# Two routing groups for three, a reordered start and end, and the first layernorm split between ScalarE and VectorE, in a fused attention and mixture-of-experts layer

## The chip, the cores and the metric

The kernel runs on one core of a Trainium2 chip. The metric is the device time of one execution in microseconds (us), the median of several runs. All data is float32.

A core has five engines that work side by side and wait for each other by semaphores: TensorE (PE, matmuls; PEld is its weight load), VectorE (DVE), ScalarE (ACT), GpSimd (POOL) and SyncE (SP, which here only issues transfers). Each works through its own queue in order, so an instruction that waits holds up all that stand behind it. Matmuls write PSUM; everything else lives in SBUF.

## The reference

x has 16 sequences of 512 tokens of 128 numbers (8192 tokens, 64 tiles of 128). Two layers follow each other, with a layernorm around each:

```python
q = silu(x @ Wq); k = silu(x @ Wk); v = x @ Wv        # 16 heads of 8
q, k = lrpe(q, theta), lrpe(k, theta)                 # [t*cos(theta*n), t*sin(theta*n)]
energy = einsum('bhnd,bhmd->bhnm', q, k) * tril       # causal, without a softmax
out = (energy @ v).reshape(b, n, d) @ Wo * sigmoid(x @ G1 @ G2)
out = (out - mean) / sqrt(var + 1e-5) * gamma + beta  # the first layernorm
x = layernorm(x + out)                                # the second
# mixture of experts: 8 experts, 2 for each token, 1280 places for each expert
shared = silu(x @ sg) * (x @ su) @ sd                 # 128 -> 1024 -> 128, all tokens
routed = the same form with 512 hidden, for the tokens of each expert, weighted, added back
x = layernorm(x + shared + routed)
```

## The kernel before

**First part: the loop over tiles.** Lines 788 to 832 go over t = -2 to 64, one tile of 128 tokens at a time. An iteration projects tile t+2 (`project`, L414: two matmuls L418 and L421 into one PSUM tile; SiLU, tanh and spreading copies on ScalarE, L425 to L441; the multiplication with cosines and sines on VectorE, L445), transposes tile t+1 (`turn_over`, L458, with four copies on ScalarE), computes the products of queries and keys of tile t (`energies`, L505, masked on VectorE, L513), the outputs of tile t-1 (`values`, L530 and L538, copied at L544), and adds tile t+1 to a running state (`remember`, L479; VectorE masks it at L488, POOL adds it at L490). Linear attention lets it carry a state instead of all earlier keys.

When the four tiles of a sequence are through, a generator `after(b)` (L547) is started. It projects with Wo (L553), gates (L557), takes the statistics of the first layernorm (L105, L107, L111; POOL raises to the power -1/2, L113), applies it with two groups of four VectorE instructions (L565, L570), and does the second layernorm (statistics, L580, and ScalarE's L584). Then it transposes the result into x1T (L600, L601) and computes the router's logits. Each `yield` in it ends one slot; `advance` runs one slot at two places of each iteration.

The shared expert is a list of 384 small steps (`feed`), 24 for each sequence: eight of `gate_half` (L137, L139) and eight of `up_half` (L150, L151), a 512-wide matmul each, and eight of `down_half` (L160, and L165 for every second one). `shared(t)` takes the next step if its sequence is released (`ready[b]`), twice an iteration. They fill TensorE's queue.

Routing (`route`, L618) runs once for each group of sequences. It is a chain of some 40 VectorE instructions over all tiles of the group, with one Exp on ScalarE (L644, which loads another activation table) and two matmuls (L690, L691). `sprinkle` deals its slots out. At its end every tile of the group owes two scatters: each an indirect transfer that POOL issues (L723), writing 128 token rows to the places of their experts in DRAM. Before a scatter, `beat` (L740), a tiny POOL instruction that reads a recent result, holds POOL back. The loop issues two scatters a tile.

After tile 64 a second loop (L838 to L856) goes on with shared steps alone, one an iteration, until the last sequences are finished, routed and scattered, with one scatter every second iteration, and 12 steps more.

**Second part.** The eight experts (L1021 to L1026, L928 to L942) load their rows (`load_expert`), blank rows that nobody filled (`clear_rows`, L893), transpose them (L904, L905) and scatter results back. What is left of `feed` then fills TensorE while, for each sequence, the two results of its tokens are loaded (`load_pair`) and added (`add_up`, L953), and the last layernorm is taken over lots of tiles (`finish_lot`, L969: L105, L107, a root, L985, ScalarE's L988, and the store). The lots are the four tiles of a sequence, single tiles for the last one.

The order of instructions on TensorE, ScalarE, VectorE and POOL is the order in which the code issues them (`manual_schedule`).

Of the kernel before, what the change touches and what calls it, by code (L numbers as in the profile page):

```python
# [13 lines left out]
ALU = mybir.AluOpType  # L14
# [33 lines left out]
def tile_kernel(  # L48
# [145 lines left out]
    groups = [(0, 6), (6, 12), (12, 16)]  # L194
    with ExitStack() as ph:
# [21 lines left out]
        with tc.manual_schedule(engines=ORDERED):  # L217
            th_row = cst.tile([1, D + HALF], F32, name="th_row")
            nc.sync.dma_start(th_row, theta.unsqueeze(0))
# [15 lines left out]
            nc.vector.memset(half_pi, math.pi / 2)  # L235
            warm = cst.tile([P, 1], F32, name="warm")
# [25 lines left out]
            nc.vector.tensor_scalar(rowi, rowi, 16, None, ALU.bitwise_and)  # L262
            bitf = cst.tile([P, 1], F32, name="bitf")
            nc.vector.tensor_copy(bitf, rowi)
            par = cst.tile([P, 2], F32, name="par")
            nc.vector.tensor_scalar(par[:, 0:1], bitf, -1.0 / 16, 1.0, ALU.mult, ALU.add)
            nc.vector.tensor_scalar(par[:, 1:2], bitf, 1.0 / 16, None, ALU.mult)
# [11 lines left out]
            pth = ps_w.tile([P, D + HALF], F32, tag="w", name="pth")  # L279
            nc.tensor.matmul(pth, ones[0:1, :], th_row, start=True, stop=True)  # L280
            th_sb = wk1.tile([P, D + HALF], F32, tag="w", name="th_sb")
            nc.scalar.copy(th_sb, pth)
# [3 lines left out]
            for vp in vpads[2:]:  # L286
                nought(vp.rearrange("p a b d -> p (a b d)"), 640)
# [3 lines left out]

            cst_tok = cst.tile([P, NC, 2, 16, 2, 8], F32, name="cst_tok")
            scratch = hp.tile([P, 10, D + HALF], F32, tag="h", name="scratch")
            turns_of = wk1.tile([P, D + HALF], F32, tag="o", name="turns_of")
            nc.vector.tensor_scalar(turns_of, pth, 1.0 / (2.0 * math.pi), None, ALU.mult)

        def angles(c, th):

            a, size, k, whole = scratch[:, c], scratch[:, NC + c], scratch[:, 8], scratch[:, 9]
            both = ((slice(0, D), pos[:, 0, c : c + 1]), (slice(D, D + HALF), pos[:, 1, c : c + 1]))
            for m, at in both:
                nc.vector.tensor_scalar(k[:, m], turns_of[:, m], at, MAGIC, ALU.mult, ALU.add)
            nc.vector.tensor_scalar(whole, k, MAGIC, -C1, ALU.subtract, ALU.mult)
            for m, at in both:
                nc.vector.scalar_tensor_tensor(a[:, m], th[:, m], at, whole[:, m], ALU.mult, ALU.add)
            nc.vector.tensor_scalar(k, k, MAGIC, -C2, ALU.subtract, ALU.mult)
            nc.vector.tensor_tensor(a, a, k, ALU.add)
            nc.vector.scalar_tensor_tensor(size, a, -1.0, a, ALU.mult, ALU.max)  # L310
            nc.vector.tensor_scalar(a, a, -PI_BELOW, PI_BELOW, ALU.max, ALU.min)
# [4 lines left out]
        def sines(c):  # L316

            for s, (from_, scale, bias) in enumerate([(scratch[:, NC + c], -1.0, half_pi), (scratch[:, c], 1.0, 0.0)]):
# [14 lines left out]
        with tc.manual_schedule(engines=ORDERED):  # L333
            angles(0, pth)
            sines(0)
            angles(1, th_sb)
            same(0)

# [3 lines left out]
            nc.gpsimd.tensor_tensor(causal[:, 0:1], scratch[:, 0, 0:1], zcol, ALU.mult)  # L342
# [13 lines left out]
            for at in (0, HALF):  # L356
                rows = causal[at : at + HALF, :]
                nc.gpsimd.affine_select(
                    rows, rows, pattern=[[1, HALF]], compare_op=ALU.is_ge, fill=0.0, base=0, channel_multiplier=-1
                )  # L360
# [53 lines left out]
        def project(t):  # L414
# [27 lines left out]
            if 0 < t < NC:  # L442
                same(t)
# [669 lines left out]
```

## Time and profile before

| what | value |
|---|---|
| median of 3 runs | 866.24 us (865.83 to 866.31) |
| the profiled execution | 866.67 us, of which its span 864.9 us |
| TensorE busy | 821.7 us (95%) |
| VectorE, ScalarE, POOL busy | 538.2 (62%), 414.5 (48%), 361.6 us (42%) |
| granted TensorE clock, mean | 0.988 |
| tiles: first projection to last (L418) | 5.0 to 358.1 us |
| last scatter issued (L723) | 521.6 us |
| experts (L1021, L1023) | 536.5 to 750.6 us |
| last matmul (L160) ends | 856.4 us |

A row of the profile by groups reads: line, engine and operation, the names out<-in with shapes, how often; busy time in us and mean duration in ns; idle time of the engine just before, and what ended it. A row of a timeline begins with start and duration in us; a wait stands in brackets at its end. A row of waits reads: who waited for whom, total us, how often, longest. Busy time by stage has the stretch, its length, then busy time and instructions of each engine, and the granted clock (PEclk, 1.00 is full speed).

### The profile page before, as it was taken

The page shows a single profiled execution, that of the slowest core. Times are in us where ns is not written, and L with a number is a line of the kernel's source. Part 1 is how long each engine was busy: PE and PEld are TensorE (multiplying, and loading weights), DVE is VectorE, ACT ScalarE, POOL GpSimd, SP SyncE. Part 2 cuts the span into 40 slices and gives each one's busy share as a digit, 9 for nine tenths or more (in the row PEclk, how much of TensorE's full clock was granted, in tenths as well). Part 3 has the DMA queues.
Part 4 walks back from the last instruction along what each step waited for, and adds up shares of the span by engine and source line. Part 5 has one row for each costly group of instructions (what it writes and reads, how often), then busy time and mean ns, then how long its engine had stood idle before and what let it go on. Part 6 is the DMA issues. An engine that isn't in the chain of part 4 may idle for free. (4 is left out here: it accounts for less than half of the span.)

```text
span 864.9 us, 25793 instructions
## 1 busy us (share of the span) xinstructions
PE 821.7 (95%) x10288; PEld 559.5 (65%) x10288; DVE 538.2 (62%) x1695; ACT 414.5 (48%) x1342; POOL 361.6 (42%) x512
## 2 busy tenths in 40 slices
PE   6899999989999999999999999999999999999996
PEld 4666667657766765756666656766777667765564
DVE  7688887789877778865533324434344444268864
ACT  5676776676566567534222221333333333324445
POOL 2233333332366676677666671333343333412110
PEclk9899999999999999999999999999999999999998
DMA  6011111111111110039000005122321210046512
GB/s 199 22 35 33 33 33 34 33 34 33 38 43 55 55 47 22 22 130 326 28 14 8 1 1 152 37 90 91 95 84 35 90 61 28 27 143 182 155 49 62
DMA packets 66395, 57.55 MB, mean 67 GB/s; under 512 B 6180, under 2 KB 55132, under 8 KB 66274
## 3 DMA queue, kind: packets, MB, share of 16 engines
q1 hardware_dynamic: 59474, 44.95, 17.0%
q0 software_dynamic: 6656, 10.69, 3.8%
q8 instruction: 81, 1.33, 0.7%
q10 hardware_dynamic: 144, 0.26, 0.1%
q14 instruction: 40, 0.33, 0.1%
HBM read 32.62 MB, written 26.48 MB: 68 GB/s over the span
## 5 line engine op out<-in xcount | busy, mean ns | idle before, releaser
L723 POOL DMA_INDIRECT xg_dram<-x,idx x128 | 128.9, 1007 | 38.7 <-issue 34.1
L934 POOL DMA_INDIRECT y_dram<-y,to x80 | 77.5, 969 | 158.4 <-ACT y L932 158.4
L151 DVE TENSOR_TENSOR h<-sl,pu 128x512 f32<-128x512 f32 x128 | 87.8, 686 | 80.9 <-PE pu L150 45.5
L137 PE MATMUL pg<-x1T,sg_sb 128*128 128x512 f32 x256 | 131.5, 595 | 1.7 <-DVE x1T L165 1.7
L139 ACT ACTIVATE sl<-pg 128x512 f32<-128x512 f32 x128 | 75.5, 594 | 119.6 <-PE pg L137 73.4
L150 PE MATMUL pu<-x1T,su_sb 128*128 128x512 f32 x256 | 130.8, 593 | 0.0
L160 PE MATMUL pd<-sd_sb,h 128*128 128x128 f32 x1024 | 122.8, 276 | 4.7 <-DVE x1T L165 4.7
L160 PEld LDWEIGHTS pd<-sd_sb,h 128*128 128x128 f32 x1024 | 119.1, 192 | 11.5 <-issue 5.7
L1026 DVE TENSOR_TENSOR eh<-esl,peu 128x512 f32<-128x512 f32 (+1 forms) x96 | 57.5, 599 | 109.7 <-PE peu L1023 96.5
L113 POOL TENSOR_TENSOR rstd<-ve,neghalf 128x4 f32<-128x4 f32 x45 | 49.3, 1095 | 125.4 <-DVE ve L111 121.0
L490 POOL TENSOR_TENSOR state<-state,add 128x128 f32<-128x128 f32 x96 | 44.1, 459 | 137.4 <-DVE add L488 131.0
L928 PEld LDWEIGHTS ped<-rd,eh 128*128 128x128 f32 x640 | 84.0, 192 | 24.6 <-issue 22.5
L513 DVE TENSOR_TENSOR et<-pe,causal 128x256 f32<-128x256 f32 x256 | 90.5, 416 | 14.5 <-PE pe L505 13.0
L1021 PE MATMUL peg<-xgT,rg 128*128 128x512 f32 (+1 forms) x192 | 84.6, 522 | 0.0
L1023 PE MATMUL peu<-xgT,ru 128*128 128x512 f32 (+1 forms) x192 | 84.4, 521 | 0.0
L928 PE MATMUL ped<-rd,eh 128*128 128x128 f32 x640 | 84.3, 275 | 0.0
L1025 ACT ACTIVATE esl<-peg 128x512 f32<-128x512 f32 (+1 forms) x96 | 50.5, 526 | 55.0 <-PE peg L1021 52.3
L150 PEld LDWEIGHTS pu<-x1T,su_sb 128*128 128x128 f32 x256 | 45.7, 190 | 44.1 <-issue 38.7
L932 ACT ACTIVATE y<-ped,wt 128x128 f32<-128x128 f32 x80 | 29.4, 368 | 84.6 <-PE ped L928 84.6
L137 PEld LDWEIGHTS pg<-x1T,sg_sb 128*128 128x128 f32 x256 | 44.3, 191 | 38.9 <-issue 33.7
L418 PE MATMUL pq<-W,xT 128*128 128x384 f32 x128 | 61.0, 560 | 4.7 <-ACT qT L467 2.5
L445 DVE TENSOR_TENSOR hat<-qk,cst_tok 128x512 f32<-128x512 f32 x64 | 44.9, 702 | 26.2 <-ACT qk L427 26.1
(176 smaller groups left out, 1272.0 us busy)
## 6 DMA issues: line engine op xcount, KB each, us to landing
y_dram<-vpad SPq DMA_DIRECT2D x16, 512.0 KB
y<-y_dram SPq DMA_DIRECT2D x32, 256.0 KB
xT<-xt SPq DMA_DIRECT2D x15, 384.0 KB
xg<-xg_dram SPq DMA_DIRECT2D x8, 660.0 KB
x<-x SPq DMA_DIRECT2D x16, 256.0 KB
o<-res SPq DMA_DIRECT2D x15, 256.0 KB
xg_dram<-x,idx POOLq DMA_INDIRECT x128
rg<-rg SPq DMA_DIRECT2D x8, 256.0 KB
```

The costliest lines, as they stand in the source:

```text
L137: nc.tensor.matmul(pg, sg_sb[:, ts(i, P)], seq, start=True, stop=True)
L139: nc.scalar.activation(sl, pg, AF.Silu)
L150: nc.tensor.matmul(pu, su_sb[:, ts(i, P)], seq, start=True, stop=True)
L151: nc.vector.tensor_tensor(h[i // half][:, i % half, :], h.pop(("s", i)), pu, ALU.mult)
L160: nc.tensor.matmul(pd, h[k][:, i - k * half, ts(c, P)], sd_sb[:, i, :], start=(i == 0), stop=(i == IS // P - 1))
L418: nc.tensor.matmul(pq[:, :, 0:24], xts[b][:, c, 0:P], W[:, 0:384].rearrange("p (h n) -> p h n", n=24), start=True, stop=True)
L513: nc.vector.tensor_tensor(et.rearrange("p s i n -> p (s i) n"), pes[a, half].rearrange("p s i n -> p (s i) n"), causal.unsqueeze(1).to_bro ...
L723: i = nc.gpsimd.indirect_dma_start(out=xg_dram[:, :], out_offset=bass.IndirectOffsetOnAxis(ap=idx[:, k, t : t + 1], axis=0), in_=x1[:, t, ...
L928: nc.tensor.matmul(pd, h[:, i, ts(c, P)], got[e][2][:, i, :], start=(i == 0), stop=(i == IR // P - 1))
L934: i = nc.gpsimd.indirect_dma_start(out=y_dram[:, :], out_offset=bass.IndirectOffsetOnAxis(ap=to[:, at : at + 1], axis=0), in_=y, in_offset ...
L1021: nc.tensor.matmul(pg[:, :n], rg_sb[:, ts(i, P)], xgTs[e][:, ds(o0, n)], start=True, stop=True)
L1023: nc.tensor.matmul(pu[:, :n], ru_sb[:, ts(i, P)], xgTs[e][:, ds(o0, n)], start=True, stop=True)
```

## The change

Several parts at once. The groups become two of eight sequences. Constants for the start are computed by fewer VectorE instructions: ScalarE makes theta times position (`linear`) and the absolute value, and the first three tiles are laid out by hand in front of the loop, which now begins at t = 1. `project` is cut into pieces for that (`products`, `squash`, `gate`, `spread`, `turn`), with unchanged content. In `after`, ScalarE applies mean and deviation of the first layernorm, and VectorE multiplies gamma and adds x for four tiles in one instruction each; a slot is added. Sequences are released to the shared steps at t+7 (they were at t+6, the first at t+10). Scatters of an iteration come ahead of `remember`, routing gets three slots an iteration where it had five, and the second loop issues two scatters in three iterations. In the second part four shared steps come ahead of the first `clear_rows` and two more between; `add_up` first adds the two results on POOL, then the sum on VectorE; the last lots are two, one and one tile; and the steps of the lots are paced over what is left of `feed`.

```diff
-    groups = [(0, 6), (6, 12), (12, 16)]
+    groups = [(0, 8), (8, 16)]
...
-            nc.sync.dma_start(th_row, theta.unsqueeze(0))
+            nc.scalar.dma_start(th_row, theta.unsqueeze(0))
...
+            linear(0, pth)
+            linear(1, pth)
...
+        def linear(c, th):
+                for m, order in both:
+                    nc.scalar.activation(
+                        scratch[:, NC + c, m], th[:, m], AF.Copy, scale=pos[:, order, c : c + 1]
+                    )
...
+        def angles(c, turns):
+            a, k = scratch[:, c], scratch[:, 8 + c % 2]
+            for m, order in both:
+                nc.vector.tensor_scalar(a[:, m], turns[:, m], pos[:, order, c : c + 1], MAGIC, ALU.mult, ALU.add)
+            nc.vector.tensor_scalar(k, a, MAGIC, None, ALU.subtract)
+            nc.vector.scalar_tensor_tensor(a, k, -C1, scratch[:, NC + c], ALU.mult, ALU.add)
+            nc.vector.scalar_tensor_tensor(a, k, -C2, a, ALU.mult, ALU.add)
+            nc.vector.tensor_scalar(k, a, -PI_BELOW, PI_BELOW, ALU.max, ALU.min)
...
+            nc.scalar.activation(scratch[:, NC + c], scratch[:, c], AF.Abs)
...
             w = wk1.tile([P, NC, D], F32, tag="w", name=f"w_{b}")
+            nb1 = small.tile([P, NC], F32, tag="nb1", name="nb1")
+            nc.vector.scalar_tensor_tensor(nb1, mv[:, :, 0], -1.0, r, ALU.mult, ALU.mult)
             for c in range(NC):
-                nc.vector.scalar_tensor_tensor(
-                    w[:, c, :], o[:, c, :], mv[:, c, 0:1], gam, ALU.subtract, ALU.mult
+                nc.scalar.activation(
+                    w[:, c, :], o[:, c, :], AF.Identity, bias=nb1[:, c : c + 1], scale=r[:, c : c + 1]
                 )
-            yield
-            for c in range(NC):
-                nc.vector.scalar_tensor_tensor(
-                    w[:, c, :], w[:, c, :], r[:, c : c + 1], x_sb[:, c, :], ALU.mult, ALU.add
-                )
+                if c == 1:
+                    yield
+            yield
+            nc.vector.tensor_tensor(w, w, gam.unsqueeze(1).to_broadcast([P, NC, D]), ALU.mult)
+            nc.vector.tensor_tensor(w, w, x_sb, ALU.add)
             yield
...
-            for t in range(-2, NT + 1):
+            products(0)
+            products(1)
+            sines(0)
+            squash(0)
+            turn(0)
...
+            spread(0)
+            gate(0)
+            linear(2, th_sb)
+            sines(1)
+            turn_over(0)
+            angles(2, turns_of)
+            remember(0)
+            squash(1)
+            turn(1)
+            spread(1)
+            gate(1)
+            energies(0)
+            products(2)
+            turn_over(1)
+            remember(1)
+            linear(3, th_sb)
+            angles(3, turns_of)
+            sines(2)
+            squash(2)
+            turn(2)
...
+            for t in range(1, NT + 1):
...
-                sprinkle(t, 2)
+                sprinkle(t, 1)
...
+                if left:
+                    scatter_behind(oTs[(t - 1) // NC][:, ds((t - 1) % NC * P, 1)])
+                    scatter_behind()
                 if 0 <= t + 1 < NT:
                     remember(t + 1)
-                if left:
-                    scatter_behind(oTs[(t - 1) // NC][:, ds((t - 1) % NC * P, 1)])
-                    scatter_behind()
...
-                sprinkle(t, 3)
+                sprinkle(t, 2)
...
-                    ready[b] = t + (6 if b else 10)
+                    ready[b] = t + 7
...
-                if waited > 1:
+                if waited > 3:
...
-                if t % 2 == 0:
-                    scatter_behind(latest[0])
+                if t % 3 > 0:
+                    scatter_behind(latest[0] if t % 3 == 1 else None)
...
         def add_up(b):
+            ys = pairs[b]
+            nc.gpsimd.tensor_tensor(ys[:, 0], ys[:, 0], ys[:, 1], ALU.add)
+            at = begun
+            yield True
+            while feed and begun < at + 4:
+                yield False
...
+                    nc.vector.tensor_tensor(rows, rows, ys[:, 0, c0:c1], ALU.add)
...
-        lots = [(b * NC, b * NC + NC) for b in range(B - 1)] + [(t, t + 1) for t in range(NT - NC, NT)]
+        lots = [(b * NC, b * NC + NC) for b in range(B - 1)] + [(NT - 4, NT - 2), (NT - 2, NT - 1), (NT - 1, NT)]
...
-            for o0, n in parts:
-                clear_rows(0, o0, n)
-            for _ in range(4):
-                feed.pop(0)[2]()
+            for n_before, cleared in ((4, parts[:2]), (2, parts[2:])):
+                for _ in range(n_before):
+                    feed.pop(0)[2]()
+                for o0, n in cleared:
+                    clear_rows(0, o0, n)
...
+            due, steps_each = 0, 9
...
+                due += len(ends) * steps_each / max(len(feed) - 2, 1)
+                for _ in range(2):
+                    if due >= 1 or not feed:
+                        due = max(due - 1, 0)
+                        an_end()
```

## The prediction

> **What bounds the kernel now.** I read the head of the page and its slices first, to see which engine the time belongs to.
>
> ```profile
> span 864.9 us, 25793 instructions
> ...
> PE 821.7 (95%) x10288; PEld 559.5 (65%) x10288; DVE 538.2 (62%) x1695; ACT 414.5 (48%) x1342; POOL 361.6 (42%) x512
> ...
> PE   6899999989999999999999999999999999999996
> PEclk9899999999999999999999999999999999999998
> ```
>
> TensorE carries the span. The change neither adds nor removes a matmul of weight (one small one joins the start), so it can only win idle time, time at a lowered clock, and stretches in which matmuls follow each other too slowly. Idle in the plain sense is 864.9 - 821.7 = 43.2 us. The busy time by stage says where that lies; I cut the span at the output projections (L553) of some sequences and at the first and last expert.
>
> ```profile
> core 0: us, PE busy (x) PEld busy (x) DVE busy (x) ACT busy (x) POOL busy (x), PEclk, DMA share, GB/s
> 0.00:98.30 98.30, 83.35 (x2019) 58.48 (x2019) 77.62 (x276) 65.60 (x288) 31.82 (x69) 0.93 0.23 69
> 98.30:165.10 66.80, 66.73 (x1528) 47.29 (x1528) 53.86 (x189) 45.00 (x183) 22.21 (x31) 1.00 0.12 33
> 165.10:214.30 49.20, 45.79 (x1015) 31.25 (x1014) 43.20 (x149) 33.41 (x127) 13.87 (x21) 1.00 0.11 33
> 214.30:309.90 95.60, 93.03 (x2047) 66.03 (x2047) 75.20 (x261) 59.68 (x244) 56.89 (x80) 1.00 0.15 47
> 309.90:381.00 71.10, 65.58 (x1408) 45.07 (x1407) 58.87 (x208) 40.36 (x147) 46.17 (x62) 1.00 0.09 28
> 757.00:865.00 108.00, 96.36 (x460) 62.41 (x458) 75.75 (x256) 47.86 (x107) 14.71 (x14) 0.97 0.41 118
> ```
>
> Idle: 15.0 us in the first 98 us, 0.1 in the clean attention stretch, 3.4, 2.6 and 5.5 in the three with routing and scatters, 11.6 behind the experts. (From 381 to 757 us only 5.2.) Busy time hides more: the same work per sequence takes longer once routing starts. The timeline of L553, one row per sequence, shows it.
>
> ```profile
> 142.92 1.06 PE L553 MATMUL po<-wo_sb,oT 128*128 128x128 f32 x8
> 165.12 1.05 PE L553 MATMUL po<-wo_sb,oT 128*128 128x128 f32 x8
> 189.58 1.16 PE L553 MATMUL po<-wo_sb,oT 128*128 128x128 f32 x8 [1.90 <-ACT vpad L441]
> 261.86 1.05 PE L553 MATMUL po<-wo_sb,oT 128*128 128x128 f32 x8
> 286.14 1.06 PE L553 MATMUL po<-wo_sb,oT 128*128 128x128 f32 x8
> ```
>
> A clean sequence takes 22.2 us (142.92 to 165.12). With routing it takes 24.5 (to 189.58); with scatters alone, 24.3 (261.86 to 286.14). The waits of TensorE name the rest:
>
> ```profile
> PE pout L538 <- issue: 6.0, 16, 0.5
> PE pd L160 <- DVE x1T L165: 4.7, 3, 1.6
> PE pst L479 <- ACT vpad L441: 3.1, 1, 3.1
> ```
>
> The first stands only beside scatters, the second at the entry to the experts (one) and in the end (two), the third at 20 us, in the start.
>
> **The change part by part.** *Two groups.* All eleven intervals from the fourth to the fifteenth L553 take 361.49 - 98.28 = 263.2 us, against 11 x 22.2 = 244.2 clean: 19.0 too many. The four with scatters alone (214.35 to 309.87, 32 scatters) hold 95.5 - 88.8 = 6.7, so 0.21 us a scatter. The two with only the first routing hold 49.2 - 44.4 = 4.8. The two with the second routing and 16 scatters hold 51.6 - 44.4 = 7.2. Counting steps by the loop's own rules, the old order routes twice and issues 52 scatters before the loop over tiles ends; the new one routes once and issues 28, and 100 come later, where TensorE runs long matmuls and POOL's queue holds nobody up. Left: 28 x 0.21 = 5.9, and one routing of 32 tiles at 3 slots a tile instead of 5. Its instructions are a third longer, but spread over eleven tiles; I take 4.1 (between 3 and 6.4, which is 4.8 scaled by 32/24). One pair of table loads for Exp (2 x 1.28 us, behind the 1.90 us stall above) leaves with the second routing. So 19.0 falls to 10.0: **-9** (from -13 to -2, if the 0.21 belongs to something that doesn't go with the scatter).
>
> *The first layernorm.* Off VectorE go 64 x 397 + 64 x 344 ns = 47 us by the row means; by busy time, pipelined, 21.6 + 18.1 = 39.7. On come, per sequence, one small instruction (0.15, as L580) and two of 128x512 (0.68 each, as L557): 16 x 1.51 = 24.2. VectorE saves 15.5. ScalarE gets 64 activations like L584, 0.88 us for two: 28 us, or 1.76 of each 22.2 us, from 67% busy to 75%. In the clean stretch TensorE was idle 0.1 us, so this is worth nothing there; near routing it helps and is inside the -9. It adds a wait: the first activation needs the small instruction, that needs POOL's power (1.10 us mean), and behind it in ScalarE's queue stand the next SiLUs, the spreads and the copies that free PSUM. Nearest row: L584 waits for L580, 16.7 us in all, about 1 us each, nearly all of it beside a busy TensorE. Price: between -1 and +16; I take **+3**. The power's result is now used half a tile later instead of a whole one, with 1.41 + 0.48 us of VectorE work between, which covers 1.1.
>
> *The start.* Each angle loses 2.9 - 1.7 = 1.2 us of VectorE (eight or nine instructions become six) and gives ScalarE 0.35 + 0.5. The third one goes ahead of the loop and the fourth's angle too; the 3.08 us stall at 20.2 us waited for exactly that chain. Walking both queues with the old durations, the fifth SiLU comes at about 24 us, where it was at 26.82. I take **-3** (-6 to +1: ScalarE is now the long queue there, and theta's transfer stands ahead of W on it, 0.37 us).
>
> *Shared steps three tiles sooner.* Sequence 0 is released at tile 11, not 14: six steps, 6 x 0.87 = 5.2 us of matmuls, come into stretches with gaps. After 56 us there are idles of 0.95 and 0.47 us, and the next 4 us run at a granted clock of 0.58. [...] The row decides: **-2.5** (-5 to +1).
>
> *Later waits.* The routing matmul's wait for L679 (1.3 us at 413 us) gets two more steps of cover: **-1.3**. At the entry to the experts L893 waits 3.82 us for its rows, with evictions L165 behind it; 1.58 + 0.58 us of TensorE idle follow. Four steps now go ahead of it and two between: **-2** (-2.2 to 0).
>
> *The end.* Thirty-odd additions of 683 ns become 16 on VectorE (-10 us) and 16 on POOL at 1.27 (as L554). [...] I count the gain. VectorE falls under 65 of 108 us, the final norms are spread over the remaining steps, and of the two L165 stalls (3.1 us) **-2.5** goes (-3.1 to +2). Behind the last matmul (856.4) four single-tile lots take turns at 1.15 us; with one left, eviction, statistics, root, reciprocal, scale and store take 2.4 + 2.5: **-3** (-3.6 to 0).
>
> *POOL after the loop over tiles.* Two scatters in three steps: 2 x 0.99 + 0.22 + about 0.35 between, 2.55 of 2.62 us, where one in two steps took 1.38 of 1.74. The last two sequences' powers queue behind that: 0 to +6, I take **+1.5**. The loop stays the same length (162 iterations for 164).
>
> Sum: -9 + 3 - 3 - 2.5 - 1.3 - 2 - 2.5 - 3 + 1.5 = -18.8. The profiled execution took 866.67 (864.9 of it the span), so 847.9; the median stands 0.4 lower: **847.5**.
>
> **Rivals.** *Only the ends gain* (0.20): the 0.21 us moves from the scatters to whatever else runs then, and half of the start is eaten by ScalarE: 866.2 - 18.8 + 9 + 2.5 = 858.9. For it: I know where those waits stand, not why. Against: the clean stretch, with all the rest present, has none.
>
> *ScalarE's new wait decides* (0.11), slower: every sequence's L584-like wait reaches TensorE. Without the +3 the sum is -21.8, so it turns from 21.8/16 = 1.36 us a sequence. The wait at 53 to 55 us (2.22) did reach it, before shared steps were there. At 2.2 all through: 866.2 - 21.8 + 35 = 879.4. Against: eight such waits from 180 to 380 us, at most two beside a TensorE stall.
>
> *POOL falls behind* (0.07): 100 scatters at 1.27 are 127 us in 130; with powers and lag the last lands some 10 us late, and the first expert's rows with it: 847.5 + 11 = 858.5.
>
> **How the numbers follow.** The forecast has 0.62. Within 0.2% is about what a measurement here can tell from nothing. Faster: 0.62 + 0.20 + 0.05 of the third = 0.87; same 0.03; slower 0.10. The unknowns of the forecast (13 to 2, -1 to 16, and the ends) span 835 to 858 if few fall the same way; with the two rivals short of no change the range is **835 to 864**.
>
> **What would show it.** L553 intervals at 22.2 outside routing, 24 beside scatters, in fewer intervals; two fewer table loads; L538's wait for "issue" at half; no L165 stall behind 757; the last matmul within 5.5 us of the end; the fifth projection before 23 us. Wrong, if L584's new neighbour heads ScalarE's waits and L418, L458 or L553 wait for ScalarE in every sequence, or if POOL's last scatter lies within 8 us of the first expert matmul.

## The result, and the profile after

The changed kernel takes 879.6 us (median, 878.5 to 881.5), the kernel before beside it 866.3 (865.8 to 867.2): a ratio of 1.0155 (95% interval 1.0132 to 1.0177). It is slower, where 847.5 was forecast, and outside the range. Later sets of runs fell on five other chips, and on the one of them where it was run the same pair stands the other way: 848.5 against 854.8 us, 0.9925 (0.9910 to 0.9940). The loss on the first is traced below to one stall; why only that chip shows it stays open. I call the chip of the first runs, and that of the first four experiments (chip 13), on which the kernel before takes 866 us, the *866 chips*, and the five others, on which it takes 854 to 855 us, the *855 chips*. The record names no chip for the first runs, so the 866 chips may be a single one; and all runs on them came ahead of all runs on the others.

The head of the page of the changed kernel on the 866 chip, with the row of TensorE's busy slices and that of its granted clock:

```profile
span 876.9 us, 25665 instructions
...
PE 829.0 (95%) x10286; PEld 564.1 (64%) x10286; DVE 513.9 (59%) x1554; ACT 436.6 (50%) x1408; POOL 383.2 (44%) x491
...
PE   6989999999999999997899898999999999998797
...
PEclk9999999999999999997998899999999999999999
```

VectorE is 24 us lighter, and it did not help. TensorE is busy 7 us longer with the same work. Between the 19th and the 25th slice, 395 to 548 us, four fall below 9, and the clock in three; the rows of before had a 9 there throughout. That stretch is the loop over tiles that follows the attention. By stage (ends of stages are the starts of the last output projection's last matmul and of the first and last gate matmul of the experts):

| us | before, 866 chip | after, 866 chip | before, 855 chip (e12) | after, 855 chip (e9) |
|---|---|---|---|---|
| start and attention, to | 381.8 | 362.5 | 370.7 | 360.9 |
| tail: loop over tiles, entry to the experts | 154.7 | 186.5 | 153.8 | 156.8 |
| experts | 213.3 | 213.3 | 213.3 | 213.3 |
| end | 115.1 | 114.6 | 115.1 | 113.7 |
| span | 864.9 | 876.9 | 852.9 | 844.7 |

(e12 and e9 ran on two different 855 chips, each beside runs of the kernel before that agree within 0.1 us in their medians.) So on the 866 chip the attention gained 19.3 us and the tail lost 31.8; on the 855 chip the gain is 9.8 and the loss 3.0. (Of the attention's figures 1 to 2 us are chance, see the start in the part after the experiments.) By the traces the tail holds 166 shared steps in both kernels: on the 866 chip it cost 0.93 us a step before and 1.12 after.

In the table by stretches of the changed kernel on the 866 chip (columns: window, length, busy time and count of TensorE, weight loads, VectorE, ScalarE, GpSimd; clock, DMA share, GB/s), the tail reads:

```profile
361.70:549.00 187.30, 167.63 (x717) 103.42 (x716) 66.29 (x154) 43.14 (x78) 117.33 (x159) 0.93 0.25 81
```

TensorE is idle for 19.7 us, and the granted clock of the stretch is 0.93. The list of waits of the run (total, times, longest) says at which matmuls:

```profile
DVE x1T L165 <- remote: 36.2, 8, 7.5
...
PE pd L160 <- issue: 15.6, 28, 1.1
```

The wait of L160 for "issue" is new: no instruction that the trace shows was late. The evictions behind those matmuls (L165) come late too, released by nothing that the trace names ("remote"). One set of eight down steps in the timeline of TensorE shows what happens:

```profile
424.57 6.08 PE L160 MATMUL pd<-sd_sb,h 128*128 128x128 f32 x53
431.14 0.49 PE L160 MATMUL pd<-sd_sb,h 128*128 128x128 f32 x3 [0.49 <-issue]
432.56 0.51 PE L160 MATMUL pd<-sd_sb,h 128*128 128x128 f32 x3 [0.92 <-issue]
433.98 0.62 PE L160 MATMUL pd<-sd_sb,h 128*128 128x128 f32 x4 [0.91 <-issue]
435.42 0.27 PE L160 MATMUL pd<-sd_sb,h 128*128 128x128 f32 x1 [0.83 <-issue]
```

53 of the 64 matmuls run at the usual 0.11 us each; the other 11 come in handfuls, one handful every 1.42 us. The set takes 11 us and not 7. Beside it, in the timeline of GpSimd:

```profile
424.89 0.97 POOL L746 DMA_INDIRECT xg_dram<-x,idx  x1 [0.30 <-issue]
425.88 0.21 POOL L763 TENSOR_TENSOR beat<-h,neghalf 128x1 f32<-128x1 f32 x1
426.25 0.99 POOL L746 DMA_INDIRECT xg_dram<-x,idx  x1 [0.16 <-issue]
427.55 0.97 POOL L746 DMA_INDIRECT xg_dram<-x,idx  x1 [0.30 <-issue]
```

Scatters stand back to back, two in 2.65 us. The beat that should space them reads the newest h, and while down steps run no new h is made, so it waits for nothing. This goes on as long as the down steps do.

The beat of the kernel before has the same gap. In one of its sets on the 866 chip the scatters follow each other every 1.38 us, behind beats that don't wait, and the set runs through:

```profile
417.57 7.31 PE L160 MATMUL pd<-sd_sb,h 128*128 128x128 f32 x64
...
421.80 0.99 POOL L723 DMA_INDIRECT xg_dram<-x,idx  x1 [0.16 <-issue]
...
423.18 0.99 POOL L723 DMA_INDIRECT xg_dram<-x,idx  x1 [0.16 <-issue]
```

So the distance inside a set is not all that differs (1.30 to 1.36 us after, 1.38 before). The scatters ahead of a set stand closer too: mostly 5 in the 7 us before it, where the kernel before has 3 or 4. Of the seven sets in the changed kernel's tail four starve badly, one a little and two not at all.

### The profile page after: what moved, and what is told of

The parts are those of the page before. It is cut to its first block, busy times and chain, and to the rows that moved or that the text cites. A ratio compares the mean times of both kernels' runs of the same rounds, so it can differ in the third digit from the quotient of the medians.

```text
span 876.9 us, 25665 instructions
## 1 busy us (share of the span) xinstructions
PE 829.0 (95%) x10286; PEld 564.1 (64%) x10286; DVE 513.9 (59%) x1554; ACT 436.6 (50%) x1408; POOL 383.2 (44%) x491
## 4 chain that ended last, share of the span: by engine, by line
PE 77%; DVE 11%; ACT 5%; issue 4%; POOL 2%; DMA 0%; DVEq 0%; ACTq 0%; POOLq 0%
PE pd L160 13%; PE pg L137 10%; PE pu L150 10%; PE ped L984 8%; PE peg L1083 8%; PE peu L1085 8%; PE pq L426 5%; PE pe L526 3%; PE pt L479 2%; PE pout L559 2%; DVE et L534 2%; PE pst L500 2%; DVE h L151 2%; DVE st L105 2%; PE po L574 1%
## 5 line engine op out<-in xcount | busy, mean ns | idle before, releaser
L160 PE MATMUL pd<-sd_sb,h 128*128 128x128 f32 x1024 | 135.3, 285 | 23.4 <-issue 15.6
L160 PEld LDWEIGHTS pd<-sd_sb,h 128*128 128x128 f32 x1024 | 127.5, 199 | 33.0 <-issue 24.1
L137 PE MATMUL pg<-x1T,sg_sb 128*128 128x512 f32 x256 | 135.9, 613 | 2.2 <-DVE h L151 0.8
L150 PE MATMUL pu<-x1T,su_sb 128*128 128x512 f32 x256 | 133.0, 602 | 0.0
L511 POOL TENSOR_TENSOR state<-state,add 128x128 f32<-128x128 f32 x96 | 53.1, 553 | 89.0 <-DVE add L509 80.1
L466 DVE TENSOR_TENSOR hat<-qk,cst_tok 128x512 f32<-128x512 f32 x64 | 47.1, 735 | 26.9 <-ACT qk L438 26.5
```

What stands on the lines that cost most here:

```text
L137: nc.tensor.matmul(pg, sg_sb[:, ts(i, P)], seq, start=True, stop=True)
L150: nc.tensor.matmul(pu, su_sb[:, ts(i, P)], seq, start=True, stop=True)
L160: nc.tensor.matmul(pd, h[k][:, i - k * half, ts(c, P)], sd_sb[:, i, :], start=(i == 0), stop=(i == IS // P - 1))
```

## The experiments

All ratios are to the kernel before on the same chip, with their 95% intervals.

**e1, the pace alone, on the kernel before** (866 chip).

```
-                if t % 2 == 0:
-                    scatter_behind(latest[0])
+                if t % 3 > 0:
+                    scatter_behind(latest[0] if t % 3 == 1 else None)
```

> The kernel before with only the new scatter pace in the second loop (two in three steps, the second of them without a beat). Theory P (the pace, alone, starves TensorE while it runs the 128-wide steps of the shared expert): the stretch from the last output projection to the first expert takes more us a step than the 155.5/168 = 0.93 of before, about 1.1, with 'issue' waits of L160, though it has some 38 steps fewer; the kernel lands at 875 to 890 us. Rival Q (it takes two groups, whose routing and powers crowd POOL and VectorE there): 862 to 868 us and at most 3 us of such waits.

Measured: 893.1 us, 1.0317 (1.0299 to 1.0336), 3 us above the range of theory P; rival Q fell. The first wait of TensorE:

```profile
PE pd L160 <- issue: 16.7, 25, 1.8
```

The second is L538's for issue, 6.1 us, as before (6.0). L160's is the one of the changed kernel, with nothing else of the change present. The tail takes 149.6 us for 128 steps, 1.17 us a step. On this chip the new pace is enough to make the stall.

**e2, the changed kernel with the old pace** (866 chip): the edit of e1 the other way.

> The changed kernel with the old pace (one scatter in two steps, each behind a beat). Theory P: L160's waits for 'issue' fall from 15.6 us to under 3 and the stretch from the last output projection to the first expert costs under 0.95 us a step. It has some 50 steps more (100 scatters at one in two), which are then missing at the end (64 left instead of 114), where the last norms lie bare: 862 to 885 us in all, to be read by stage. Rival Q: the waits stay above 10 us.

Measured: 868.4 us, 1.0022 (1.0013 to 1.0030). No wait for issue at L160 is left; the tail runs at 0.92 us a step (199.4 us, 216 steps). But 100 scatters at one in two steps make it 50 steps longer, so that only 58 are left for the end, which still takes 89.5 us: 1.5 us a step. There the additions and norms have too few matmuls to lie beside: the last matmul ends 26 us ahead of the end of the span, where the changed kernel has 4.7. The old pace saves the starving and pays at the end.

**e3, a beat ahead of each scatter, and e4, a beat that follows the down steps too** (866 chip; changed kernel).

```
-                    scatter_behind(latest[0] if t % 3 == 1 else None)
+                    scatter_behind(latest[0])
```

> The changed kernel with its pace, but a beat (on the latest product of the shared expert) ahead of every scatter, not of every second one. Theory P (rate): nothing but POOL's 0.2 us a scatter more, 877 to 884 us. Rival G (scatters without a beat, issued back to back, are what hurts): the waits for 'issue' fall under 5 us, 855 to 868 us.

Measured: 876.4 us, 1.0127 (1.0107 to 1.0147), with 7.5 us of issue waits in the trace, which is of its fastest run (872.8 us). Neither expectation was met in full. The second beat reads the same h as the first and spaces little. By e3's rows (a scatter of 0.99 us, a beat of 0.21 and 0.21 of idle ahead of a scatter) I estimate about 1.4 us from scatter to scatter where no beat waits, as in the kernel before (1.38), and the down steps starve all the same, for 7.5 us in 13 waits where the changed kernel has 15.6 in 28. Distance inside the set is therefore not enough to explain the stall; the pace ahead of it goes with it.

```
                 nc.vector.tensor_tensor(base[:, t, :], pd, x1[:, t, 0:D], ALU.add)
+                latest[0] = base[:, t, 0:1]
```

> The changed kernel, where the beat also follows the evictions of the down steps (L165), so that POOL can't run ahead through the eight down steps of a sequence. Rival G' (the burst through the down steps, whose beats are all satisfied, is what hurts): waits for 'issue' under 5 us, 850 to 862 us. Theory P (mean rate, POOL over 95% taken, wherever the scatters lie): 875 to 884 us.

Measured: 868.0 us, 1.0015 (1.0003 to 1.0027); the tail takes 173.5 us, 13 less than with the change as it is, and 10.0 us of issue waits remain. One added line, which only spaces scatters in the down steps, takes back 11.6 of 13.3 us of the loss. It does not clear the stall, and neither expectation was met: of each two scatters the second still has no beat of its own.

**e5, e4 with the additions of the end on VectorE again**, paced as before the change (855 chip).

> The changed kernel with a beat that also follows the down steps, and with the sums over the two experts' rows back on VectorE, paced as before the change; the new lots and their pacing stay. Theory A (GpSimd's additions at the end hold VectorE's tiny operations, and through them ScalarE's SiLUs and TensorE, so moving them cost more than it gained): the tiny product nb of a lot is back at about 0.15 us from up to 1.23, the two stalls of 2.7 and 4.7 us of the down steps behind a late eviction are gone, the end (last expert's row to the end of the span) falls from 113 to about 108 us, and the time from 868.0 to 860 to 865. Theory B (the additions gain where they are, VectorE is the bound at the end as the prediction held): the time rises to 870 to 874.

Measured: 854.7 us, 1.0000 (0.9989 to 1.0011). The end takes 122.5 us; with the additions on GpSimd (e9, another 855 chip) it takes 113.7, with as many shared steps (108). Theory A fell. The edit moves the additions and gives them their old pacing at once, so it does not say which of the two costs the 8.8 us. In the timeline of TensorE in e5 the stalls of the down steps behind a late eviction are not gone but three, of which the first:

```profile
769.12 6.59 PE L160 MATMUL pd<-sd_sb,h 128*128 128x128 f32 x32 [4.13 <-DVE x1T L165]
```

They sum to 11.4 us, against 6.7 in two stalls in e9. Half of theory A's premise did hold, and is in the last section: the tiny product of the last norms, up to 1.23 us beside GpSimd's additions, never exceeds 0.163 us here.

**e6, the kernel before with the new first layernorm alone, and e18, the changed kernel with the old one** (855 chips). The edit is that of `after` in the diff, once put in and once taken out.

> The kernel before with one part of the change: ScalarE scales the first layernorm, VectorE applies gamma and the sum over four tiles at once. The prediction's term: between -1 and +16, +3 taken. With 16 sequences, VectorE saves about 1 us a sequence and gains nothing where it isn't the bound; ScalarE takes four more instructions of 0.27 us a sequence. If the four products on ScalarE delay its exponentials and evictions, the sequence period grows by up to 1 us and the time to 870 to 882; if they lie in its idle time, 864 to 868. From the changed kernel's attention, which ran 19 us shorter with this part in it, 864 to 868 is expected.

> The changed kernel with the first layernorm on VectorE again, as before the change: one part undone. The part alone gained 0.12% (0.02 to 0.23%) on the kernel before. If it is worth the same here: where before takes 855 us, 848 to 851 beside 848.5 for the changed kernel. If the prediction's +3 for ScalarE's new wait was right: 844 to 847.

Measured: e6 853.9 us, 0.9988 (0.9977 to 0.9998). e18 847.6 us, 0.9916 (0.9900 to 0.9933), where the changed kernel with all its parts has 0.9925 (0.9910 to 0.9940) on another 855 chip. By the one the part gains 0.9 us, by the other nothing that can be told from zero. The prediction's price of 3 us for ScalarE's new wait is not there. By stage the part does act: the eleven intervals from the fourth to the fifteenth output projection take 253.9 us in e6 for 256.8 in the kernel before (e12), and 251.8 in e18 for 247.7 in the changed kernel (e9). The tail gives some of it back: 1.1 us in e6, and 3.1 between e18 (153.7) and e9 (156.8). Why the tail does so is open.

**e8, plain rows**: the changed kernel with a plain transfer of the same 128 rows in place of each scatter, from GpSimd's queue and behind the same beats. The rows go to fixed places, so the experts work on other rows (855 chip).

```
-            i = nc.gpsimd.indirect_dma_start(out=xg_dram[:, :], ...)
+            nc.gpsimd.dma_start(rows, x1[:, t, :])
```

> The changed kernel with each indirect scatter replaced by a plain transfer of the same 128 rows from GpSimd's queue, at the same places and behind the same beats; the rows go to fixed places and not to their experts', so the experts work on other rows. It tells what in a scatter starves TensorE in the down steps. If it is the rows' traffic itself (the same bytes and about as many descriptors on the same DMA engines), the issue waits of 15 us and the lengthening of the tail remain: 875 to 880. If it is the making of the indirect descriptors on GpSimd, which holds it for 1 us each, they go: the waits for issue in the down steps fall below 3 us, the tail to about 160 us, and the time to 850 to 862.

Measured: 843.5 us, 0.9872 (0.9855 to 0.9889), no issue wait at the down steps. This looked like the answer, and was not: e5 and e6, on the same chip, had none either, though e5 keeps the fast pace and e6 the scatters inside the attention, where before had 6.0 us of such waits. So the changed kernel itself had to be run on such a chip.

**e9, the changed kernel again, and e10, plain rows beside it** (855 chip).

> The changed kernel itself, unaltered, in a further set of runs: the kernel before took 866.3 us beside the first four experiments and 854.8 us beside the next three, which ran on another chip, and in the latter no wait of TensorE for issue is left on any line, not in the attention either. Theory P1 (the fast pace of the scatters costs what it costs on every chip): the ratio to before is again 1.013 to 1.018, with 10 to 16 us of waits for issue at the down steps. Theory P2 (the pace only costs where TensorE's instructions come late, and the chips differ in that): where the kernel before takes about 855 us, the waits for issue are gone, the tail after the last output projection takes 150 to 158 us instead of 187, and the ratio is 0.985 to 0.995; where before takes 866, as P1.

> The changed kernel with each indirect scatter replaced by a plain transfer of the same rows from GpSimd's queue (the rows go to fixed places, so the experts work on other rows), beside the changed kernel itself on the same chip. If the indirect scatters starve TensorE: where the changed kernel shows 10 us or more of issue waits, this one shows under 3 and is 25 to 35 us faster. Where the changed kernel shows none, this one is within 6 us of it: 3 to 5 us less for down steps that no longer wait behind late evictions.

Measured: e9 848.5 us, 0.9925 (0.9910 to 0.9940); e10 843.1 us, 0.9860 (0.9843 to 0.9876). P2 holds. In e9's list of waits none of TensorE's matmuls waits for issue. Its tail, in the table by stretches:

```profile
360.80:517.70 156.90, 152.40 (x713) 94.85 (x712) 66.74 (x154) 42.62 (x76) 117.65 (x159) 0.99 0.30 95
```

A set of down steps, from its timeline of TensorE:

```profile
416.39 7.31 PE L160 MATMUL pd<-sd_sb,h 128*128 128x128 f32 x64
```

And GpSimd beside that set:

```profile
416.81 0.97 POOL L746 DMA_INDIRECT xg_dram<-x,idx  x1 [0.30 <-issue]
...
418.17 0.99 POOL L746 DMA_INDIRECT xg_dram<-x,idx  x1 [0.16 <-issue]
```

The scatters are as close as on the 866 chip, to the hundredth, and a scatter has the same duration (median 992 ns in both). Only TensorE differs: all 64 matmuls run through in 7.31 us. With plain rows e10 is 5 us faster than e9, nearly all of it in the tail (152.2 against 156.8 us). So on this chip indirect scatters cost the tail some 4 us more than plain transfers at the same places; that the same tail takes 30 us more on the 866 chip is another matter.

**e12, the kernel before with a trace, and e13, the pace alone** (855 chip).

> The kernel before, unaltered, with a trace on the chip of this set. On a chip where it takes about 855 us: no waits for issue on the attention's products (6.0 us of them where it took 866), the last output projection at 367 to 371 us, as in the kernel with the new layernorm alone (368.0), and the tail to the experts at 153 to 156 us. On a chip where it takes 866: as the trace of before.

> The kernel before with the new pace of the scatters alone, which took 3.2% more on the chip where before takes 866 us. If TensorE's instructions come late on such a chip only, it takes within 0.4% of before where before takes 855 us, 853 to 858; if back-to-back scatters cost on every chip, 872 to 882. Where before takes 866 us, again 890 to 895.

Measured: e12 854.4 us; its span is in the table above. The whole difference between the two kinds of chip, 12.0 us of span, lies in the attention (11.1) and the tail (0.9). The timeline of the output projection shows where half of the attention's share is:

```profile
213.71 1.08 PE L553 MATMUL po<-wo_sb,oT 128*128 128x128 f32 x8
...
303.23 1.05 PE L553 MATMUL po<-wo_sb,oT 128*128 128x128 f32 x8
```

Those are the four intervals with scatters alone: 89.5 us, 22.4 a sequence, where the prediction read 95.5 from the 866 chip and a clean sequence has 22.2. Another 3.2 us are in the last interval, and 1.5 ahead of the fourth projection, where runs of one kernel differ as much. The 6.0 us that L538 waits for issue on the 866 chip are absent here, and with them nearly all of the 0.21 us a scatter. e13 took 861.7 us, 1.0081 (1.0060 to 1.0103): between the two expectations. There is no issue wait. The faster pace leaves 38 steps fewer for the tail, which is 23.2 us shorter than in e12, and 38 more for the end, which is 30.7 longer. Of the 7.4 between them one wait in the tail makes 5.7:

```profile
PE pu L150 <- DVE h L151: 5.7, 1, 5.7
```

So on the 855 chips the pace costs the kernel before one wait and a little more, but no starving. The tail takes 130.5 us, against 149.6 for the same kernel on the 866 chip (e1), and the end 145.8 on both: the stall is worth 19 us there.

**e11, e15, e17, three groups with the old pace**: the changed kernel with e4's line and these two edits (three 855 chips).

```
-    groups = [(0, 8), (8, 16)]
+    groups = [(0, 6), (6, 12), (12, 16)]
...
-                if t % 3 > 0:
-                    scatter_behind(latest[0] if t % 3 == 1 else None)
+                if t % 2 == 0:
+                    scatter_behind(latest[0])
```

> The changed kernel with three groups instead of two, one scatter every second step, and a beat that follows the down steps too: scatters never back to back, 44 of the 128 instead of 28 inside the attention loop, so that 180 steps lie before the experts and 96 are left for the end. If two groups are what gains in the attention, it ends 5 to 10 us later than the changed kernel's; if the pace was what lost, the tail runs at 0.92 us a step. Together: 850 to 857 where before takes 866 us, a ratio of 0.980 to 0.990; if three groups cost as much as the grouping was thought to gain (9 us), 858 to 863.

> The changed kernel with three groups, one scatter every second step and a beat on the down steps too. Where before takes 855 us: 841 to 846 again, a ratio of 0.985 to 0.989. Where before takes 866 us: no two scatters are back to back, so the starving stays at or below that of before, and the ratio is 0.982 to 0.992.

> The changed kernel with three groups, one scatter every second step and a beat on the down steps too. Where before takes 855 us: 841 to 846 again, a ratio of 0.985 to 0.989. Where before takes 866 us: no two scatters are back to back, so the starving stays at or below that of before, and the ratio is 0.982 to 0.992.

Measured: 843.2, 843.0 and 842.0 us; 0.9869 (0.9848 to 0.9891), 0.9869 (0.9842 to 0.9897), 0.9857 (0.9834 to 0.9879). In e11 the attention ends at 362.5 us, 1.6 later than in e9 (its fourth output projection already started 2.0 later), where 5 to 10 were expected if two groups are what gains; the tail takes 167.2 us for 184 steps, 0.91 a step; the end 97.7. It beats both kernels there, by 11 to 12 us and by 5. On the 866 chips it was not run. The output projections of e11 from the fourth to the fifteenth:

```profile
98.59 1.05 PE L575 MATMUL po<-wo_sb,oT 128*128 128x128 f32 x8
...
345.28 1.05 PE L575 MATMUL po<-wo_sb,oT 128*128 128x128 f32 x8
```

The eleven intervals take 246.7 us, here and in e15 and e17. With two groups they take 247.6 or 247.7 in all seven runs with a trace on 855 chips that keep the new layernorm. Three groups are 1 us better, not 9 worse.

**e14, e16, e19, plain rows on further chips**, to learn what in a scatter starves TensorE.

> The changed kernel with each indirect scatter replaced by a plain transfer of the same rows to fixed places, so that the experts work on other rows. Where before takes 855 us: 842 to 845 again. Where before takes 866 us it tells what starves TensorE: if it is the indirect descriptors made on GpSimd, under 3 us of issue waits and 850 to 858; if it is the rows' traffic, 10 us or more and 872 to 880.

> The changed kernel with each indirect scatter replaced by a plain transfer of the same rows to fixed places, so that the experts work on other rows. Where before takes 855 us: 842 to 845 again. Where before takes 866 us it tells what starves TensorE: if it is the indirect descriptors made on GpSimd, under 3 us of issue waits and 850 to 858; if it is the rows' traffic, 10 us or more and 872 to 880.

> The changed kernel with each indirect scatter replaced by a plain transfer of the same rows to fixed places, so that the experts work on other rows. Where before takes 855 us: 842 to 845 again. Where before takes 866 us it tells what starves TensorE: if it is the indirect descriptors made on GpSimd, under 3 us of issue waits and 850 to 858; if it is the rows' traffic, 10 us or more and 872 to 880.

Measured: 843.6, 843.9 and 844.0 us; 0.9864, 0.9869, 0.9876. All three fell on 855 chips and repeat e8 and e10. The question they were for stays open.

## Why the prediction was wrong, point by point

**The step that failed** is the one on GpSimd after the loop over tiles, together with the clause that moves the scatters there: "100 come later, where TensorE runs long matmuls and POOL's queue holds nobody up". I took +1.5, from 0 to +6, for GpSimd's own queue. The tail lost 31.8 us on the 866 chip and 3.0 on an 855 chip. GpSimd's queue is innocent: the last scatter starts at 532.0 us, the first expert matmul at 549.0. What is hit is TensorE. And not all matmuls there are long: the down steps are 128 wide, 64 of them and their 64 weight loads in 7 us, and those are the ones that starve (15.6 us of issue waits). The trace of before had shown such a wait at 6.0 us (L538 waiting for "issue", only beside scatters), and I priced it per scatter, at 0.21 us, as if it belonged to the attention. On the 866 chip it goes with the pace of the scatters where short matmuls run. The change moved 24 of them behind the attention and raised the pace there, from one in two steps (1.74 us) to two in three (2.6 us). The beats of before let the scatters through at 1.38 us inside the down steps without harm, so a set at that distance alone does not starve. e1 shows that the pace is enough by itself, and e2 that the old pace takes the stall away; e3 and e4 lessen it. Through what the scatters hold TensorE up is not shown.

**The attention** went better than forecast, and for another reason. Over the eleven intervals from the fourth to the fifteenth projection the 263.2 us became 248.2 (-15.0) on the 866 chip, and 256.8 became 247.7 (-9.1) on the 855 chip; the forecast for groups, layernorm and shared steps together was -8.5. The -9 was put down to one routing and 24 scatters fewer, and its size is met by luck: with three groups, two routings and 42 scatters the intervals take 246.7 us (e11, e15, e17). What gained on the 855 chips is that an interval with routing became cheap: 24.5 to 26.0 us in e12, 22.9 to 23.2 in e9, and in e11 no interval is over 23.0. With the old layernorm in the changed kernel (e18) they are 23.0 to 24.8 again. So some 4 of the 9.1 us go with the first layernorm's move to ScalarE (4.1 by e18, 2.9 by e6). The other 5 belong to the rest of the change, of which routing at three slots a tile and scatters ahead of the state's update are in the loop; no run parts them. On the 866 chip the 28 scatters left in the loop, for which I had counted 5.9 us, cost next to nothing: the two intervals with them take 299.39 to 344.16, 44.8 us, which is 22.4 each. That they now stand ahead of the step that updates the state may be why; it was not tried alone.

**The first layernorm**: +3 taken, -0.9 (e6) to about 0 (e18) measured over the whole, with the gain in the attention and a loss in the tail that is told under e6 and e18. ScalarE's new wait exists (11.1 us over 13 waits), but the 16.7 us that L584 waited for its own small product fall to 1.7 (L607 in the changed kernel), so it is no addition. The slower rival, which made this wait decide, had its number met (879.4) and its mechanism not.

**The start**: -3 taken; no gain that can be told from chance. The fourth output projection comes 2.3 us sooner in the first pair of traces, but over all traces it starts between 96.4 and 98.3 us with the old start (five traces) and between 96.0 and 99.6 with the new one (fifteen). In the first pair the fifth projection's matmul moved from 24.66 to 23.10; a new wait of 2.8 us for the scaling of wo, which I had not queued, stands against it. The granted clock of the first 96 us rose from 0.93 to 0.98, as the earlier release of shared steps was meant to do, and that too is not seen at the fourth projection. The -2.5 for that release was my estimate from two idles of 0.95 and 0.47 us in the trace of before and the 4 us at a clock of 0.58 behind them; no run shows the term, and the higher clock is what the traces show in its place.

**Wait of the routing matmul**: gone, as forecast (1.3). The shortening at the entry to the experts can't be seen below the tail's loss.

**The end**: -5.5 taken, -0.5 and -1.5 measured, with six fewer steps in it (5.2 us at 0.87). Behind the last matmul 8.5 us became 4.7, the term of -3. But the stalls behind L165, which were to go, grew: from the timeline of TensorE after, on the 866 chip,

```profile
799.79 5.46 PE L160 MATMUL pd<-sd_sb,h 128*128 128x128 f32 x32 [2.70 <-DVE x1T L165]
...
828.12 5.47 PE L160 MATMUL pd<-sd_sb,h 128*128 128x128 f32 x32 [4.70 <-DVE x1T L165]
```

7.4 us where there were 3.1. I had counted the gain of fewer additions on VectorE in full. In the trace of before L445, with a median of 0.69 us, once took 1.31 beside an addition of GpSimd:

```profile
39.38 1.31 DVE L445 TENSOR_TENSOR hat<-qk,cst_tok 128x512 f32<-128x512 f32 x1 [1.40 <-ACT qk L427]
...
38.87 1.27 POOL L554 TENSOR_TENSOR x<-x,bet 128x512 f32<-128x512 f32 x1
```

Of the work at the end I had taken only the new additions for exposed to that, which was not shown. VectorE after, in the stretch of the two stalls:

```profile
788.12 0.15 DVE L1045 SCALAR_TENSOR_TENSOR nb<-mv,rstd 128x4 f32<-128x4 f32 x1
789.39 1.23 DVE L1045 SCALAR_TENSOR_TENSOR nb<-mv,rstd 128x4 f32<-128x4 f32 x1
```

The second stands beside GpSimd's addition of 128x512 at 789.05 us, the first beside one of its powers of 128x4. Of the fifteen 128x4 products of L1045 the six that stand beside such an addition took 0.67 to 1.23 us, the nine others 0.15 or 0.16, and ScalarE's scaling behind the one at 801.84 us (1.23) waited 1.09 us for it. Yet by e5, where none of them exceeds 0.163 us, the additions on GpSimd, with their pacing, are still the better side (an end of 113.7 us for 122.5): the longer products are there and do not decide. That the new spreading of the norms over the steps makes the stalls is what I suspect; no run changed it alone.

**The two kinds of chip.** On the 855 chip the direction of the forecast came out, at a third of its size: faster by 0.75%, where it said 2.2%. The gain lies in the attention, as it said, but not by the grouping. The nearness of 848.5 to the forecast 847.5 is chance, since before is 12 us lower there.

**What stays open.** The 866 chips' matmuls wait when scatters stand close (15.6 us of L160 for issue), the 855 chips' do not (none in e9). Two differences go with it in the records: late evictions with a releaser that the trace doesn't show (L165 behind "remote", 36.2 us, none in e9), and pages without a single time from issue to landing of a DMA, where those of the 855 chips have them (2.3 us for a scatter in e9). And since the 866 chips are one or two and were measured first, it is not shown that the chip itself makes the difference. Whether TensorE's instructions came late, or its signals, or whether the recording takes part, no run tells apart. Plain rows on an 866 chip would be the first step.

## What to carry to other kernels

Where a chip shows waits of TensorE for "issue" beside indirect scatters, as the 866 chips do, they need not stay at the place and size where they are first seen (here 6.0 us at L538 before, 15.6 at L160 after): count the scatters per microsecond where they are to go, over more than the few microseconds of one step, and look which matmuls run there. A beat that spaces transfers must follow something that advances in every phase; one that reads the output of one kind of step lets everything through while the other kind runs (here beats of 0.21 us without a wait, and scatters 1.30 to 1.36 us apart). And where a forecast rests on a wait that nothing in the trace explains, look whether it is there on a second chip before building on its size. When several parts change at once, a sum that comes out does not confirm its terms: here the largest, the grouping, turned out to be worth nothing on the 855 chips when three groups were put back.

## What the runs showed of the hardware that I had not expected

- The same program took 866.3 us in the runs on one chip or two and 854.2 to 854.9 on five others, and a change was 1.6% slower on the first and 0.75% faster on one of the others. A scatter took the same time on both (medians of 992 to 994 ns); for the change, it is one stall in the tail that makes most of the difference.
- In the four sets of the changed kernel that starve most, TensorE got through 47 to 53 of 64 matmuls at the usual 0.11 to 0.12 us each, then took one to four of them at a time, mostly 0.7 or 1.4 us apart.
- On the 866 chips a set of down steps ran through in 7.31 us with five scatters in it, four of them 1.38 us apart (before), and e2, with one scatter in two steps, has no wait of L160 for issue; e3, with two in three steps and a beat ahead of each as in e2, has 7.5 us of them.
- In the tail on the 866 chip, with 19.7 us of idle in it, the granted clock was 0.93 (0.74 from 400 to 420 us, 0.83 from 460 to 500, 0.99 from 440 to 460); on the 855 chip, with 4.5 us of idle (e9), it was 0.99.
- The 128x4 product on VectorE (L1045) took 0.15 or 0.16 us in nine places and 0.67 to 1.23 in the six beside GpSimd's 128x512 additions (the changed kernel on the 866 chip).
